# Taking the first 32 gathers of a two-layer graph network from the raw features instead of the normalised table

## The chip, the cores and the metric

The kernel runs on one core of one Trainium2 chip. The metric is the device time of one execution in microseconds; lower is better.

## The reference

The inputs are node features x (12500 nodes, 32 features, float32) and 200000 edges, each a source `src` and a destination `dst`, sorted by `dst`. Two residual layers follow each other. Cut to what matters:

```python
h = maximum(layernorm(x), 0)              # eps 1e-5, no gain
out_norm = rsqrt(maximum(count of src, 1))
in_norm  = rsqrt(maximum(count of dst, 1))
agg = segment_sum((h * out_norm[:, None])[src], dst)
x = x + agg * in_norm[:, None] @ W + b

h = maximum(layernorm(x), 0)
a = concat([h[dst], h[src] - h[dst]]) @ W1 + b1     # then relu,
m = relu(relu(relu(a) @ W2 + b2) @ W3 + b3) @ W4 + b4
x = x + segment_sum(m, dst) / maximum(count of dst, 1)
```

The edge attributes are not used.

## The kernel before

**Edges and chunks.** Edges lie in tiles of 128 (one per partition), and four tiles make a chunk of 512 edges (`TPC`, line 34); there are 391 chunks. `src_i` holds the source numbers, one column per tile (line 151), and `dst_i` the destinations. A row of a table is fetched for each edge of a tile by one indirect DMA on POOL, which takes one column of numbers (the helper `gather`, lines 247 to 250). POOL starts these in the order of the program, and does little else.

**Opening (lines 154 to 243).** x is loaded in four pieces of 32 nodes per partition on SP's queue, while ACT's queue loads `src_i`, `dst_i` and the small inputs. POOL makes constants. DVE normalises each piece (lines 228 to 242: sum, mean, difference, square, variance, with the root on ACT), and SP writes it to the table `tab_h` in DRAM, which has a 33rd column of ones. Its rows start at 48 (`OFF`), so that the numbers used for it are `src_j`, the sources plus 48.

**Degrees and early gathers (lines 279 to 361).** The out-degree of each node is counted on PE, in 196 batches of eight tiles, from one-hot matrices that DVE compares into being (lines 318 and 335). The table with the normalisation by out-degree, `tab_hn`, can only be written after that (lines 346 to 356). So that POOL is not idle meanwhile, the first 64 chunks (`EARLY`, line 57) are gathered from `tab_h`, without the out-degree: 256 gathers into `rows_early`, let go chunk by chunk as the batches go by (lines 324 to 330).

**First layer (lines 581 to 777).** Chunks 64 to 299 are gathered from `tab_hn` (944 gathers, tile `rows`, eight buffers of a chunk each) and summed by destination on PE with one-hot matrices (`sum_rows`). The last 91 chunks are not gathered: their edges are counted into matrices and multiplied with `tab_hn` held on the chip (`count_edges`, `multiply`). The 64 early chunks come in between: `scale_rows` (lines 631 to 667) is a generator that is advanced once per iteration of the loop over m (line 754), and a new one is begun every third iteration. Its stages are: load of a row of numbers; a one-hot on DVE; a matmul that looks up the factors 1/sqrt(degree) (line 643); four masked sums on DVE that pick the factor of each edge (line 650), the multiplication with `rows_early` (line 654) and the split into three bfloat16 terms; then the sum by destination. When a block of nodes has all its sums, `update_nodes` (lines 450 to 506) forms the new x and the second layer's tables `tab_i` and `tab_j`.

**Second layer (lines 782 to 926).** 1563 gathers from `tab_j` (tile `gj`) feed the four matmul layers on pairs of chunks. They can start when `tab_j` is complete.

**Order.** The engines' queues are filled in program order (the schedule is manual). Indirect DMAs take turns over eight completion semaphores, so that the ninth waits until the first has landed.

Of the kernel before, what the change touches and what calls it, by code (L numbers as in the profile page):

```python
# [8 lines left out]
F32 = mybir.dt.float32  # L9
# [3 lines left out]
AF = mybir.ActivationFunctionType  # L13
OP = mybir.AluOpType
AX = mybir.AxisListType

P = 128
N_NODES = 12500
N_EDGES = 200000
D = 32  # L20
HID = 64
EPS = 1e-5
# [3 lines left out]
OFF = 48  # L26
# [7 lines left out]
TPC = 4  # L34
CHUNK = TPC * P
NCH = -(-N_EDGES // CHUNK)
NTR = -(-N_EDGES // P)
NT = NCH * TPC
# [14 lines left out]
HG, HT = 2, 4  # L53
AHEAD_HG = 3


EARLY = 4 * GRP * J
LATER = 3
QE = EARLY // (GRP * J)

# [20 lines left out]
def gnn_kernel(  # L83
# [20 lines left out]
    nc = tc.nc  # L104
# [24 lines left out]
    def parts(rows):  # L129

        return rows.rearrange("(p j) c -> p j c", p=NPART)
# [6 lines left out]
    rows_early = early.tile([P, EARLY, TPC, D + 1], F32, name="rows_early")  # L138
# [12 lines left out]
    src_i = mp.tile([P, NT], I32, name="src_i")  # L151
# [4 lines left out]
    pieces = [slice(j, j + PC) for j in range(0, P, PC)]  # L156
    for at in pieces:
        nc.sync.dma_start(xp[:, at, :], parts(xa)[:, at, :])
    nc.scalar.dma_start(src_i, src_t)
    nc.scalar.dma_start(dst_i, dst_t)  # L160

    o = dst.offset + DIR * CHUNK
# [41 lines left out]
    nc.scalar.dma_start(w1s[D:, :HID], b1.rearrange("(o c) -> o c", o=1))  # L204
    nc.gpsimd.memset(w1s[D:, HID:], 0.0)

    fixed = ctx.enter_context(tc.tile_pool(name="fixed", bufs=1, space=bass.MemoryType.PSUM))
# [18 lines left out]
    for at in pieces:  # L228
        h, a = hx[:, at, :D], xp[:, at, :]
        m = fp.tile([NPART, PC], F32, name="la_m", bufs=2)  # L230
# [7 lines left out]
        sd = fp.tile([NPART, PC], F32, name="la_sd", bufs=2)  # L238
# [4 lines left out]
        nc.sync.dma_start(parts(tab_h[OFF:, :])[:, at, :], hx[:, at, :])  # L243
    first.close()
    src_j = stay.tile([P, NT], I32, name="src_j")

    def gather(tile_ap, table, col):
        nc.gpsimd.indirect_dma_start(  # L248
            out=tile_ap, out_offset=None, in_=table,
            in_offset=bass.IndirectOffsetOnAxis(ap=col, axis=0))  # L250

    def gather_chunk(rows, table, g):
        for t in range(min(TPC, NTR - g * TPC)):
            c = g * TPC + t
            gather(rows[:, t, :], table, src_j[:, c : c + 1])
# [23 lines left out]
    with tc.tile_pool(name="deg", bufs=3) as hp, tc.tile_pool(  # L279
        name="deg_ps", bufs=1, space=bass.MemoryType.PSUM  # L280
# [28 lines left out]
        nc.scalar.activation(turned_hi, hi_ps, AF.Copy)  # L309
        nc.sync.dma_start(hi_row.rearrange("(b t) e -> t b e", t=P), turned_hi.rearrange("t (b e) -> t b e", e=P))  # L310
        deg_ps = pp.tile([P, PART], F32, name="deg_ps")
        gathered, batches = 0, list(range(0, NTR, HG * HT))

        def one_hots(name, k, width, b):

            hot = hp.tile([P, HG, width, HT], BF16, name=name)
            n = min(HG, (NT - b) // HT)
            nc.vector.tensor_tensor(
                hot[:, :n], hl[:, k, b : b + n * HT].rearrange("p (g t) -> p g t", t=HT)[:, :, None, :].to_broadcast(
                    [P, n, width, HT]), lane_g[:, None, :width, :].to_broadcast([P, n, width, HT]), op=OP.is_equal)  # L320
            return hot

        for b in batches:
            to = min(EARLY, -(-EARLY * (b // (HG * HT) + AHEAD_HG) // len(batches)))
            if to > gathered:
                c = slice(gathered * TPC, to * TPC)
                nc.vector.tensor_scalar(src_j[:, c], src_i[:, c], OFF, None, op0=OP.add)
                for g in range(gathered, to):
                    gather_chunk(rows_early[:, g], tab_h[:, :], g)
                gathered = to  # L330
            hi = one_hots("hi", 0, PART, b)
            lo = one_hots("lo", 1, P, b)
            for t in range(b, min(NTR, b + HG * HT)):
                g, i = divmod(t - b, HT)
                nc.tensor.matmul(deg_ps, lo[:, g, :, i], hi[:, g, :, i], start=(t == 0), stop=(t == NTR - 1))
        nc.vector.tensor_scalar(src_j[:, EARLY * TPC :], src_i[:, EARLY * TPC :], OFF, None, op0=OP.add)
        deg = hp.tile([P, PART], F32, name="deg", bufs=1)
        nc.scalar.activation(deg, deg_ps, AF.Copy)
        turned = pp.tile([PART, P], F32, name="turned")
# [2 lines left out]
        sd = hp.tile([PART, P], F32, name="sd", bufs=1)  # L342
# [3 lines left out]
        for at in pieces:  # L346
            h = hx[:PART, at, :D]
# [77 lines left out]
    with tc.tile_pool(name="flag", bufs=1) as fp, tc.tile_pool(  # L425
        name="flag_ps", bufs=1, space=bass.MemoryType.PSUM
# [154 lines left out]
    with tc.tile_pool(name="e0", bufs=8) as sp, tc.tile_pool(name="nu", bufs=1) as np_, tc.tile_pool(  # L581
        name="direct", bufs=1) as dp, tc.tile_pool(name="e0_ps", bufs=1, space=bass.MemoryType.PSUM) as pp, tc.tile_pool(
        name="nu_ps", bufs=1, space=bass.MemoryType.PSUM) as np_ps:


        sums = Sums(np_, D3, "acc", (QE, QD, NQ - 1), (QE, QD), lambda q: ("_e", 2) if q < QE else ("_t", 3) if q < QD else ("_d", 3))
        hots, rows_of, group_ps, running, updates = {}, {}, {}, [], []
# [23 lines left out]
        def hot_ahead(g, name="hot", bufs=AHEAD + 4):  # L611
            hots[g] = one_hots(sp, rel_h[:, g * TPC : (g + 1) * TPC], W, name, bufs)

        def sum_rows(g):
            k, i = divmod(g, GRP)
            if i == 0:
                group_ps[k] = pp.tile([D3, SPAN], F32, name="ps_late" if g >= EARLY else "ps_early")
            ps, rows, hot = group_ps[k], rows_of.pop(g), hots.pop(g)
            for t in range(TPC):
                nc.tensor.matmul(  # L620
                    ps[:, STEP * i : STEP * i + W], rows[:, t, :], hot[:, t // 2, :, t % 2], start=(i == 0 and t == 0),
                    stop=(i == GRP - 1 and t == TPC - 1), skip_group_check=True)

        def add_rows(g):

            k, i = divmod(g, GRP)
            if i == GRP - 1:
                sums.add(slice(0, D3), P * k, group_ps.pop(k))
                added(range(k * GRP, (k + 1) * GRP))

        def scale_rows(g):

            row = sp.tile([PART, CHUNK], F16, name="srow", bufs=2)
            nc.sync.dma_start(row, bass.AP(
                tensor=hi_row.tensor, offset=hi_row.offset + g * CHUNK, ap=[[0, PART], [1, CHUNK]]))
            yield
            turned = sp.tile([PART, CHUNK], BF16, name="sturned", bufs=2)
            nc.vector.tensor_scalar(turned, row, part_s[:PART], None, op0=OP.is_equal)
            yield
            ps = pp.tile([P, TPC, P], F32, name="look")  # L640
            for t in range(TPC):
                for k in range(3):
                    nc.tensor.matmul(
                        ps[:, t, :], turned[:, t * P : (t + 1) * P], rn3[:, k], start=(k == 0), stop=(k == 2))
            yield
            w = factors[g % 2]
            for t in range(TPC):
                c = g * TPC + t
                mask = sp.tile([P, P], F32, name="mask", bufs=2)
                nc.vector.scalar_tensor_tensor(  # L650
                    mask, lanes_s, lo_early[:, c : c + 1], ps[:, t, :], op0=OP.is_equal, op1=OP.mult,
                    accum_out=w[:, t : t + 1])
            scaled = ps[:, 0, :].rearrange("p (t c) -> p t c", t=TPC)
            nc.vector.tensor_tensor(
                scaled, rows_early[:, g, :, :D], w[:, :, None].to_broadcast([P, TPC, D]), op=OP.mult)
            rows = rows_of[g] = sp.tile([P, TPC, D3], BF16, name="rows_scaled", bufs=2)
            nc.scalar.activation(rows[:, :, 3 * D :], rows_early[:, g, :, D:], AF.Copy)
            for k in range(3):
                part = rows[:, :, k * D : (k + 1) * D]
                nc.scalar.activation(part, scaled, AF.Copy)  # L660
                if k < 2:
                    nc.vector.tensor_sub(scaled, scaled, part)
            hot_ahead(g, "hot_e", 2)
            yield
            sum_rows(g)
            yield
            add_rows(g)


        table = dp.tile([P, PART, P], BF16, name="table")  # L670
# [111 lines left out]
    with tc.manual_schedule(), tc.tile_pool(name="prep", bufs=3) as prep, tc.tile_pool(name="e1", bufs=3) as ep, tc.tile_pool(name="fn", bufs=2) as fp, tc.tile_pool(  # L782
        name="p1_ps", bufs=2, space=bass.MemoryType.PSUM
# [146 lines left out]
    with tc.If(bad > 0):  # L930
        sums0 = dram.tile([NROW, D + 1], F32, name="sums0")
        sums1 = dram.tile([NROW, D], F32, name="sums1")
        with tc.tile_pool(name="gp", bufs=1) as gp, tc.tile_pool(name="ge", bufs=1) as ge, tc.tile_pool(
            name="ge_ps", bufs=1, space=bass.MemoryType.PSUM
# [108 lines left out]
            c = gp.tile([P, NBLK], F32, name="g_c")  # L1043
# [39 lines left out]
```

## Time and profile before

| What | Value |
|---|---|
| Median of 3 runs | 4330.28 us (4326.65 to 4355.74) |
| The profiled execution | 3552.55 us |
| Its span, first to last instruction | 3550.7 us |
| POOL busy | 2616.8 us (74%) |
| PE busy | 2630.5 us (74%) |
| DVE busy | 1669.8 us (47%) |
| ACT busy | 1103.2 us (31%) |
| Mean granted TensorE clock | 0.812 |
| First gather of `tab_h` starts | 48.56 us |
| First gather of `tab_hn` starts | 375.85 us |
| First gather of `tab_j` starts | 1572.77 us |
| Last gather starts | 3517.76 us |

The profile shows one execution, which was shorter than the timed runs. In it a line such as "L248 POOL DMA_INDIRECT" stands for the line of the kernel, the engine and the operation; then follow the tile that is written and what it is made from, the count, the busy time, the mean duration, and the idle time of the engine before it with what ended it. The line of all gathers is that of the helper, so they are told apart by their tiles.

### The profile page before, as it was taken

Reading aid. Unit: us, or ns where it says so; the run is one execution under the profiler, and the core shown is the slowest. Engines: PE = TensorE matmul, PEld = TensorE weight load, DVE = VectorE, ACT = ScalarE, POOL = GpSimd, SP = SyncE. Lnnn points to the kernel's source line nnn. Section 1 sums busy time; section 2 is a strip of 40 time slices with the busy share of each in tenths; the row PEclk is TensorE's granted clock in tenths of the full one; section 3 lists DMA queues with packets and bytes.
Section 4 is the critical chain, followed back from the end, with each engine's and each line's share of the span. In section 5 each row is a group of like instructions: output and inputs, shape, how many; then the busy total and the mean of one; then the engine's idle time right before and its main releaser. Section 6 shows DMA issues by size and latency. Waiting matters only on the chain. (4 is left out here: it accounts for less than half of the span.)

```text
span 3550.7 us, 50481 instructions
## 1 busy us (share of the span) xinstructions
PE 2630.5 (74%) x18596; PEld 1780.9 (50%) x18596; DVE 1669.8 (47%) x4150; ACT 1103.2 (31%) x2552; POOL 2616.8 (74%) x2782
## 2 busy tenths in 40 slices
PE   3871567777777777637888788877788877887787
PEld 2650355555555555514555555544455545554455
DVE  8995456667666665313333333333333333333333
ACT  0002355656656655301212222222212222222212
POOL 3777777777777777767777777777777777777775
PEclk9999998888888888657767877778867788778878
DMA  4113111111211111212222222222222222222221
GB/s 88 15 15 76 24 28 31 32 35 33 38 30 34 33 34 27 45 34 59 61 61 62 61 61 61 61 59 60 61 61 62 61 61 61 61 58 61 61 61 32
DMA packets 238327, 173.61 MB, mean 49 GB/s; under 512 B 157666, under 2 KB 186562, under 8 KB 238074
## 3 DMA queue, kind: packets, MB, share of 16 engines
q0 software_dynamic: 88416, 79.16, 12.4%
q1 hardware_dynamic: 131306, 85.26, 8.8%
q10 hardware_dynamic: 18352, 5.89, 0.9%
q8 instruction: 150, 2.46, 0.3%
q14 instruction: 103, 0.84, 0.1%
HBM read 157.18 MB, written 12.92 MB: 48 GB/s over the span
## 5 line engine op out<-in xcount | busy, mean ns | idle before, releaser
L248 POOL DMA_INDIRECT gj<-tab_j,src_j x1563 | 1474.9, 944 | 493.8 <-issue 414.8
L248 POOL DMA_INDIRECT rows<-tab_hn,src_j x944 | 891.8, 945 | 287.7 <-issue 200.5
L742 ACT ACTIVATE count<-count_ps 128x429 bf16<-128x429 f32 x1089 | 545.0, 525 | 368.7 <-PE count_ps L741 347.1
L845 PE MATMUL p<-ident,gj 128*128 128x128 f32 x784 | 243.6, 351 | 400.6 <-DMA gj<-tab_j,src_j 398.8
L878 DVE TENSOR_TENSOR h<-p,b3n 128x512 f32<-128x512 f32 x196 | 135.3, 690 | 811.5 <-PE p L875 811.5
L875 PE MATMUL p<-w3s,h 128*128 128x64 f32 x3128 | 483.0, 319 | 0.0
L875 PEld LDWEIGHTS p<-w3s,h 128*128 128x128 f32 x3128 | 453.9, 231 | 50.2 <-issue 41.2
L866 ACT ACTIVATE h<-p,b2s 128x512 f32<-128x512 f32 x391 | 247.3, 683 | 739.5 <-PE p L863 739.5
L741 PE MATMUL count_ps<-oh,lo 128*128 128x429 bf16 x1089 | 433.1, 409 | 47.2 <-ACT count L742 33.1
L845 PEld LDWEIGHTS p<-ident,gj 128*128 128x128 f32 x784 | 118.0, 161 | 662.4 <-issue 641.4
L696 PEld LDWEIGHTS <-table 128*128 128x128 bf16 x4508 | 352.3, 109 | 132.2 <-issue 74.8
L696 PE MATMUL st<-count,table 128*128 128x104 bf16 (+1 forms) x4508 | 414.9, 233 | 0.1
L620 PE MATMUL ps_late<-hot,rows 128*97 128x128 bf16 x944 | 166.3, 255 | 306.7 <-DMA rows<-tab_hn,src_j 243.7
L893 PEld LDWEIGHTS ps<-hot,h 128*64 128x64 f32 x3126 | 277.5, 193 | 170.1 <-issue 157.0
L248 POOL DMA_INDIRECT rows_early<-tab_h,src_j x256 | 246.7, 964 | 124.4 <-issue 53.3
L853 ACT ACTIVATE h<-p 128x512 f32<-128x512 f32 x196 | 117.0, 597 | 689.4 <-PE p L849 689.4
L849 PE MATMUL p<-turned,ai 128*64 128x512 f32 x782 | 322.3, 915 | 0.0
L893 PE MATMUL ps<-hot,h 128*64 128x128 f32 x3126 | 306.4, 361 | 0.5 <-DVE h L878 0.5
L685 DVE TENSOR_TENSOR oh<-keys,kept 128x858 bf16<-128x858 f16 x546 | 291.7, 590 | 7.0 <-PE count_ps L741 6.9
L620 PEld LDWEIGHTS <-rows 128*97 128x97 bf16 x944 | 103.5, 138 | 361.5 <-DMA rows<-tab_hn,src_j 293.3
L863 PE MATMUL p<-h,w2s 64*128 64x512 f32 x782 | 263.9, 755 | 0.0
L829 DVE TENSOR_TENSOR turned<-row,kept 128x512 f32<-128x512 f16 x391 | 249.8, 680 | 25.1 <-PE p L849 20.3
(186 smaller groups left out, 2426.2 us busy)
## 6 DMA issues: line engine op xcount, KB each, us to landing
row<-rel_row SPq DMA_DIRECT2D x195, 256.0 KB
gj<-tab_j,src_j POOLq DMA_INDIRECT x1563
rows<-tab_hn,src_j POOLq DMA_INDIRECT x944
ai<-tab_i SPq DMA_DIRECT2D x195, 64.0 KB
srow<-hi_row SPq DMA_DIRECT2D x64, 98.0 KB
rows_early<-tab_h,src_j POOLq DMA_INDIRECT x256
tab_j<-nu_aij SPq DMA_DIRECT2D x24, 128.0 KB
tab_i<-nu_aij SPq DMA_DIRECT2D x24, 128.0 KB
```

The costliest lines, as they stand in the source:

```text
L248: nc.gpsimd.indirect_dma_start(out=tile_ap, out_offset=None, in_=table, in_offset=bass.IndirectOffsetOnAxis(ap=col, axis=0))
L620: nc.tensor.matmul(ps[:, STEP * i : STEP * i + W], rows[:, t, :], hot[:, t // 2, :, t % 2], start=(i == 0 and t == 0), stop=(i == GRP - 1 ...
L685: nc.vector.tensor_tensor(oh[:, k, :n], keys[:, k, None, i : i + 2].to_broadcast([P, n, 2]), count_h[:, :n], op=OP.is_equal)
L696: nc.tensor.matmul(ps[:, : tiles * WD], table[:, h, :], c[:, :tiles, h, :], start=(h == 0), stop=(h == PART - 1))
L741: nc.tensor.matmul(ps[:, :n], lo[:, i % TPC // 2, :, i % 2], oh[:, k, :n, i % 2], start=True, stop=True)
L742: nc.scalar.activation(counts[g][:, t, a:b, :], ps[:, :n].rearrange("p (h d) -> p h d", d=WD), AF.Copy)
L829: nc.vector.tensor_tensor(turned, v["row"][:, k], part_f.to_broadcast([P, CHUNK]), op=OP.is_equal)
L845: nc.tensor.matmul(p1[:, t, :], v["gj"][:, t].rearrange("p k c -> p (k c)"), ident, is_transpose=True, start=(t == 0), stop=False, skip_gr ...
L849: nc.tensor.matmul(p1[k * HID : (k + 1) * HID].rearrange("p t e -> p (t e)"), v["ai"][:, k], v["turned"][k], start=False, stop=True, skip_ ...
L863: nc.tensor.matmul(p2s[k], w2s[s, :], v["h1"][s, :], start=True, stop=True)
L875: nc.tensor.matmul(p3[:, k * TPC + t, :], v["h2"][k][:, t * P : (t + 1) * P], w3s, start=True, stop=True)
L893: nc.tensor.matmul(ps[k * HID : (k + 1) * HID, o : o + W], v["h3"][:, k * TPC + t, :], v["hot"][k][:, t, :], start=(i == 0 and t == 0), st ...
```

## The change

The first eight chunks (32 gathers) are taken from x itself, `xa`, as soon as the first 32 columns of `src_i` are there, which are loaded by a DMA of their own. These gathers are put on POOL's queue behind its constants, ahead of all others. The remaining 56 early chunks are gathered from `tab_h` as before. What the raw rows lack, layer normalisation, is done edge by edge in `scale_rows`: the mean is taken off and the square formed in the stage of the one-hot, the variance and the root come in the stage of the matmul, and the reciprocal of the root is multiplied into the factor of the edge. The maximum with 0 is put into the multiplication, for all 64 early chunks.

```diff
+RAW = 8
...
-    nc.scalar.dma_start(src_i, src_t)
+    for c in (slice(0, RAW * TPC), slice(RAW * TPC, NT)):
+        nc.scalar.dma_start(src_i[:, c], src_t[:, c])
     nc.scalar.dma_start(dst_i, dst_t)
...
+    nc.gpsimd.memset(rows_early[:, :RAW, :, D:], 1.0)
+    for c in range(RAW * TPC):
+        gather(rows_early[:, c // TPC, c % TPC, :D], xa, src_i[:, c : c + 1])
...
-        gathered, batches = 0, list(range(0, NTR, HG * HT))
+        gathered, batches = RAW, list(range(0, NTR, HG * HT))
...
-            to = min(EARLY, -(-EARLY * (b // (HG * HT) + AHEAD_HG) // len(batches)))
+            to = min(EARLY, RAW + -(-(EARLY - RAW) * (b // (HG * HT) + AHEAD_HG) // len(batches)))
...
-        nc.vector.tensor_scalar(src_j[:, EARLY * TPC :], src_i[:, EARLY * TPC :], OFF, None, op0=OP.add)
+        for c in (slice(0, RAW * TPC), slice(EARLY * TPC, NT)):
+            nc.vector.tensor_scalar(src_j[:, c], src_i[:, c], OFF, None, op0=OP.add)
...
             nc.vector.tensor_scalar(turned, row, part_s[:PART], None, op0=OP.is_equal)
+            h = rows_early[:, g, :, :D]
+            if g < RAW:
+                m = sp.tile([P, TPC], F32, name="raw_m", bufs=2)
+                nc.vector.tensor_reduce(m, h, AX.X, OP.add)
+                nc.vector.tensor_scalar(m, m, 1.0 / D, None, op0=OP.mult)
+                nc.vector.tensor_sub(h, h, m[:, :, None].to_broadcast([P, TPC, D]))
+                square = sp.tile([P, TPC, D], F32, name="raw_sq", bufs=2)
+                nc.scalar.activation(square, h, AF.Square)
             yield
+            if g < RAW:
+                nc.vector.tensor_reduce(m, square, AX.X, OP.add)
+                nc.vector.tensor_scalar(m, m, 1.0 / D, EPS, op0=OP.mult, op1=OP.add)
+                sd = sp.tile([P, TPC], F32, name="raw_sd", bufs=2)
+                nc.scalar.activation(sd, m, AF.Sqrt)
...
-            nc.vector.tensor_tensor(
-                scaled, rows_early[:, g, :, :D], w[:, :, None].to_broadcast([P, TPC, D]), op=OP.mult)
+            if g < RAW:
+                nc.vector.reciprocal(m, sd)
+                nc.vector.tensor_tensor(w, w, m, op=OP.mult)
+
+            nc.vector.scalar_tensor_tensor(
+                scaled, h, 0.0, w[:, :, None].to_broadcast([P, TPC, D]), op0=OP.max, op1=OP.mult)
```

The definition of `gather` moves up with its first use.

More of the change, by code (lines that the diff above doesn't have):

```diff
@@ L205, in gnn_kernel, with gather @@
     nc.gpsimd.memset(w1s[D:, HID:], 0.0)
+    def gather(tile_ap, table, col):
+        nc.gpsimd.indirect_dma_start(
+            out=tile_ap, out_offset=None, in_=table,
+            in_offset=bass.IndirectOffsetOnAxis(ap=col, axis=0))
+    nc.gpsimd.memset(rows_early[:, :RAW, :, D:], 1.0)
+    for c in range(RAW * TPC):
+        gather(rows_early[:, c // TPC, c % TPC, :D], xa, src_i[:, c : c + 1])
     fixed = ctx.enter_context(tc.tile_pool(name="fixed", bufs=1, space=bass.MemoryType.PSUM))
@@ L245, in gnn_kernel @@
     src_j = stay.tile([P, NT], I32, name="src_j")
[L247 to L250, printed above, removed]
     def gather_chunk(rows, table, g):
```

## The prediction

> **What bounds the kernel now.** I read the page first: busy times and costliest groups.
>
> ```profile
> PE 2630.5 (74%) x18596; PEld 1780.9 (50%) x18596; DVE 1669.8 (47%) x4150; ACT 1103.2 (31%) x2552; POOL 2616.8 (74%) x2782
> ...
> L248 POOL DMA_INDIRECT gj<-tab_j,src_j x1563 | 1474.9, 944 | 493.8 <-issue 414.8
> L248 POOL DMA_INDIRECT rows<-tab_hn,src_j x944 | 891.8, 945 | 287.7 <-issue 200.5
> ...
> L248 POOL DMA_INDIRECT rows_early<-tab_h,src_j x256 | 246.7, 964 | 124.4 <-issue 53.3
> ```
>
> There are 2763 gathers. Each keeps POOL 0.94 us, and most of the idle time ahead of them is issue. POOL's list of waits (engine and line, what it waited for: total us, times, longest) shows where it truly waited:
>
> ```profile
> POOL rows_early L248 <- DMA b3n<-in_b: 44.2, 1, 44.2
> POOL gj L248 <- DVE turned L829: 17.8, 1, 17.8
> ```
>
> So there are two real gaps: 44.2 us before the first gather, 17.8 us before the second layer. Everything else runs at one pace: the rows gathers start from 375.85 to 1554.05 us, 943 steps, 1.249 us each (0.94 plus 0.30 of issue). POOL's stream sets the end, and a gather that moves into the first gap takes 1.249 us off, if nobody else becomes late. Next, the timeline of the opening (start, duration, engine, line):
>
> ```profile
> 4.22 0.14 POOL L205 MEMSET w1s<- 1x64 f32 x1
> ...
> 48.56 1.10 POOL L248 DMA_INDIRECT rows_early<-tab_h,src_j  x1 [44.20 <-DMA b3n<-in_b]
> ...
> 61.23 0.94 POOL L248 DMA_INDIRECT rows_early<-tab_h,src_j  x1 [2.84 <-DVE hi L318]
> ```
>
> POOL is free from 4.36 us. The gather at 48.56 needs `tab_h` and `src_j`. The ninth, at 61.23, waits 2.84 us: the built program has it wait for the landing of the first, which is late behind the 1.6 MB load of x for the residual. The timeline where the normalised table is written shows what DVE does to POOL:
>
> ```profile
> 267.82 1.23 DVE L355 TENSOR_TENSOR hx<-hx,terms 98x1024 f32<-98x1024 f32 x1 [1.15 <-ACT terms L353]
> 267.90 1.97 POOL L248 DMA_INDIRECT rows_early<-tab_h,src_j  x1 [0.30 <-issue]
> ...
> 270.17 0.94 POOL L248 DMA_INDIRECT rows_early<-tab_h,src_j  x1 [0.30 <-issue]
> 270.19 1.23 DVE L355 TENSOR_TENSOR hx<-hx,terms 98x1024 f32<-98x1024 f32 x1 [1.15 <-ACT terms L353]
> ```
>
> A gather that starts just behind L355 takes 1.97 us; one that starts just ahead of it takes 0.94. The four writes of `tab_hn` (L356, SP) are issued between 272.57 and 290.52 us. Last, the timeline around the seam to the first layer:
>
> ```profile
> 375.85 0.94 POOL L248 DMA_INDIRECT rows<-tab_hn,src_j  x1 [0.30 <-issue]
> ...
> 378.25 0.16 PEld L620 LDWEIGHTS <-rows 128*97 128x97 bf16 x1 [36.89 <-DMA rows<-tab_hn,src_j]
> ```
>
> PE has been waiting since 341.36 for rows that POOL cannot fetch before its early gathers are through. That wait is the cover for the change.
>
> **What the Trainium skill says.** "SBUF — State Buffer", section Who interferes with whom: a DVE instruction with two SBUF inputs contends with a GpSimd instruction that reads SBUF, so do the two-port modes of copies and tensor_scalar, and the one issued first goes ahead. The trace agrees: L355 has two SBUF inputs and delayed four of eight gathers, by 0.93 us on average; the gathers at L336 (tensor_scalar) and L368 (cast) lost 0.72 and 0.65; L348, whose second input is in PSUM, delays none. "DMA: Bandwidth & Descriptors", section Anatomy of one DMA: a fixed cost of about 2 us, mostly the receipt of the write. The trace has 2.4 us from the gather at 375.85 to PE's use at 378.25.
>
> **The change part by part.**
>
> Start of the raw gathers: POOL's constants end at 4.36, and the new memset of 32 elements is about 0.2 by the 0.32 of the memset of 128 (L175). The numbers' DMA is issued by about 1.2 us. Its landing isn't shown; the load of all of `src_i` had landed by 8.16, when ACT's L187, which waits for it, went on. Bounds 4.6 and 8.2; I take 5.2, as 16 KB need little beyond the fixed cost.
>
> The 32 gathers: 32 x 1.249 = 40.0 us. In the way are DVE's twelve two-input operations of 1.23 us (L233, L234, L241 for each of four pieces, 8.34 to 42.74). At L355's average (half of them, 0.93) that is 12 x 0.46 = 5.6. Of the four integer operations of 0.97 us (L300 to L303, 44.0 to 48.0) three still find raw gathers, 3 x 0.7 = 2.1. End: 5.2 + 40.0 + 7.7 = 52.9. Bounds: walking the gathers through DVE's intervals, with one let in between two operations that follow each other, gives 50.4; with none let in, 58.1. DVE lost nothing to gathers at 270.19, so I leave its chain as it is; if each of its sixteen operations waited 0.94, that is 15 us, which cover as below.
>
> So the first gather of `tab_h` starts at 52.9 instead of 48.56, 4.3 us late (1.8 to 9.5), with 32 fewer to do. The 2.84 us stall stays, as eight gathers still fall into the load of x; without it the gain grows by 2.8. POOL's gain: 40.0 - 4.3 = 35.7 us (30.5 to 41.0).
>
> Passing it on: the first rows gather moves from 375.85 to 340.2. `tab_hn` is ready at about 292.5 (290.5 plus the fixed cost), a cover of 47.7 us that holds the 15 us, too. `src_j` comes at one chunk in 196/56 x 1.09 = 3.8 us against POOL's 5.0. PE is ready at 341.36, the rows land at 342.6. From there POOL's stream is the same, and the 17.8 us before the second layer stay.
>
> Added work, eight times, at the durations of the same operations in the node update (L481 to L490): DVE two sums of 0.286, two scalings 0.170, one difference 0.293, one reciprocal 0.171, one product about 0.17, 1.55 us, 12.4 in all; ACT a Square 0.309 and a root 0.205, 4.1 in all. No table load comes with them: the built program has one, as before. The new multiplication costs what the old did (0.292 at L491 against 0.297 at L654). This falls into the first 120 us of the stage:
>
> ```profile
> 378.00:800.00 422.00, 306.41 (x3015) 226.59 (x3016) 259.61 (x820) 245.19 (x626) 319.00 (x339) 0.88 0.17 31
> ```
>
> (columns: PE, PEld, DVE, ACT, POOL busy). DVE is busy 62%, ACT 58%, so 12.4 and 4.1 us fit; without that cover they would cost 12 us. No rows gather took over 1.06 us, so small differences such as L484's cost POOL 0.11 at most, 0.9 in all; I take 0.
>
> Other queues: ACT's has one DMA more, 0.4 us before its wait to 8.16, hidden there. SP's has none more. In the built program new waits on the raw gathers stand at DVE's L429, before the first `srow` load on SP and at PE's matmul of L437, since `src_i`'s memory is reused; they ask for the first 32 landings only, some 260 us past. Cost 0.
>
> Sum: 3550.7 - 35.7 = 3515.0 of span, 3516.9 of the execution's 3552.55. The median of the runs, 4330.28, is 1.219 times that execution, and the profile doesn't say where the 778 us are. If the opening keeps its pace, the gain stays about 36; if everything is stretched alike, it is 43.5. I take 36: **4294 us**.
>
> **Rivals.** (1) The gain is hidden anyway. In the timed runs PE may be slower: its clock was 1.00 up to 378 us, 0.77 in the second layer. In the degree loop PE needs 0.90 of each 1.09 us batch. If a batch takes over 1.33 us (47.7/196 more), rows wait for `tab_hn` instead of POOL; from 1.52 (83.3/196 more) nothing is left. Against it: the loop comes first, at full clock. Time 4330.
>
> (2) Everything is stretched: 4330.28 - 43.5 = 4287, or 4280 at the upper bound of the gain. For it: one factor explains the 778 us; against it: no view shows it.
>
> (3) Slower: the chain DVE, ACT, DVE, ACT, DVE in `scale_rows`. DVE is in order; if it waits for the Square or the root behind ACT's count copies, the one-hots behind it are late, then PE, then the row buffers. Spare are 8 buffers x 5.0 = 40 us and PE's own waits (243.7 less 36.1 of 1089 us, some 22 in 120 us). With x us lost per chunk, 8x must pass 62 to cost anything, 98 to eat the gain (x = 12), 141 for 1% (x = 18, 4373). Against it: the same pair in the node update costs DVE little:
>
> ```profile
> DVE nu_m L486 <- ACT nu_t L485: 22.7, 25, 4.3
> ```
>
> 0.9 us a time, and an iteration lies between the stages.
>
> (4) The raw gathers don't run ahead: numbers at 8.2 and DVE shutting POOL out, end near 62; gain 25 or less, 4305 to 4312.
>
> **How the numbers follow.** Main case 0.60 (4287 to 4300), hidden 0.19 (4310 to 4335), stretched 0.11 (4278 to 4287), slower 0.05, late start 0.05. The runs before spread over 29 us. Below 1% is about what a measurement of this kernel can tell from no change, and 1% is 43.3 us: faster takes the stretched case and a sixth of the main one, 0.21; slower 0.05; the rest, 0.74, is within 1%. The range 4272 to 4332 leaves out some 0.05 below and 0.14 above.
>
> **What would show it.** Raw gathers from about 5 us, some of 1.5 to 2 us; first gather of `tab_h` near 53; first rows gather near 340; PE's wait of 36.9 at L620 nearly gone; 17.8 kept. A rows gather later than 350, or PE waits that grow beside the raw chunks, would prove me wrong.

## The result and the profile after

The changed kernel takes 4297.46 us (median of 13 runs, 4289.65 to 4317.1), the kernel before 4329.29 us beside it (13 runs, 4315.13 to 4357.79). The ratio is 0.9929, 95% interval 0.9909 to 0.9948: some 32 us faster, where 36 were forecast.

One thing must be known to read what follows. The first profile of the kernel before took 3552.55 us, the timed runs 4330. In the experiments this gap went with the chip: on one chip all 35 runs of the kernel before, and the single one on another, took 3550 to 3558 us; on a third all 12 took 4347 to 4370, and the timed runs (4315 to 4358) are like these. The third chip was met for one pair of experiments only, so that it always has this pace isn't shown. I call them **the 3550 pace** and **the 4350 pace**. The profile that the prediction was worked from is at the first; the timed runs above, and the profile of the changed kernel that belongs to them, are at the second. That execution took 4293.07 us, its span is 4291.3 us, the mean granted clock 0.757. So what it shows against the first profile is the change and the pace together, and the experiments have to part them.

From its page, the busy times and the groups of the gathers (busy, mean ns of one | idle time before them and what ended most of it):

```profile
PE 2813.3 (66%) x18596; PEld 1846.0 (43%) x18596; DVE 1680.5 (39%) x4199; ACT 1108.3 (26%) x2568; POOL 2616.7 (61%) x2783
...
L211 POOL DMA_INDIRECT gj<-tab_j,src_j x1563 | 1474.5, 943 | 859.8 <-issue 443.6
L211 POOL DMA_INDIRECT rows<-tab_hn,src_j x944 | 890.7, 944 | 624.8 <-issue 234.2
...
L211 POOL DMA_INDIRECT rows_early<-tab_h,src_j x224 | 211.3, 943 | 151.6 <-DVE src_j L334 84.8
```

A gather still keeps POOL 0.94 us. But the idle time ahead of the rows gathers has gone from 287.7 to 624.8 us and that of the gj gathers from 493.8 to 859.8: at this pace POOL waits for others through both layers, and its share of the span is 61%, not 74%. The opening is as forecast. Its timeline on POOL (start, duration):

```profile
4.42 0.16 POOL L215 MEMSET rows_early<- 128x32 f32 x1
5.92 1.10 POOL L211 DMA_INDIRECT rows_early<-in_xa,src_i  x1 [1.33 <-DMA src_i<-in_src_t]
7.32 1.75 POOL L211 DMA_INDIRECT rows_early<-in_xa,src_i  x1 [0.30 <-issue]
...
51.00 0.94 POOL L211 DMA_INDIRECT rows_early<-in_xa,src_i  x1 [0.30 <-issue]
52.24 0.95 POOL L211 DMA_INDIRECT rows_early<-tab_h,src_j  x1 [0.30 <-DVE lo L325]
```

The gathers of x run from 5.92 us, some of them stretched to 1.6 to 1.9 us, and the first of `tab_h` starts at 52.24. POOL's list of waits (total us, times, longest) tells what happens at the seam to the first layer:

```profile
POOL rows_early L211 <- DVE src_j L334: 84.8, 17, 6.0
...
POOL rows L211 <- PE c_ps L451: 62.0, 1, 62.0
...
POOL gj L211 <- DMA row<-rel_row: 24.2, 1, 24.2
```

Two new things stand here. The early gathers of `tab_h` wait for their numbers, 84.8 us in all, so it is the degree loop that leads and not POOL; and the first gather of `tab_hn` waits 62.0 us after POOL is through with the early ones. The wait of 44.2 us in the opening is gone.

Names in the views of the 4350 pace need caution. A trace records the events of semaphores, the counters by which engines and DMAs tell each other that something is done, and from these events the views infer what ended a wait. The first profile holds 63128 such records, this one 20047; on the semaphores of the gathers they are 16.0 a gather there and 3.7 here. No instruction is missing at this pace (50481 in the first profile and in run 6 below, of the same kernel), but two thirds of the events are. So many waits at this pace are put down to "remote" (an event whose sender is not found) or "issue" (no event found), and a name alone proves little.

### The profile page after: what moved, and what is told of

Read it like the earlier page. It is cut to its first block, busy times and chain, and to the rows that moved or that the text cites. A ratio compares the mean times of both kernels' runs of the same rounds, so it can differ in the third digit from the quotient of the medians.

```text
span 4291.3 us, 50527 instructions
## 1 busy us (share of the span) xinstructions
PE 2813.3 (66%) x18596; PEld 1846.0 (43%) x18596; DVE 1680.5 (39%) x4199; ACT 1108.3 (26%) x2568; POOL 2616.7 (61%) x2783
## 4 chain that ended last, share of the span: by engine, by line
PE 31%; another core or an unknown queue 11%; issue 10%; POOL 6%; DVE 4%; ACT 1%; DMA 0%; ACTq 0%; DVEq 0%; POOLq 0%
PE p L900 8%; POOL gj L211 6%; PE p L888 6%; PE p L874 5%; PE ps L918 4%; PE p L870 3%; PE st L721 1%; PE count_ps L766 1%; DVE hot L575 1%; DVE h L903 1%; DVE turned L854 1%; ACT count L767 1%; PE kept L831 1%; PE ps_late L628 0%
## 5 line engine op out<-in xcount | busy, mean ns | idle before, releaser
L211 POOL DMA_INDIRECT gj<-tab_j,src_j x1563 | 1474.5, 943 | 859.8 <-issue 443.6
L211 POOL DMA_INDIRECT rows<-tab_hn,src_j x944 | 890.7, 944 | 624.8 <-issue 234.2
L766 PE MATMUL count_ps<-oh,lo 128*128 128x429 bf16 x1089 | 468.4, 442 | 384.4 <-issue 182.6
L721 PE MATMUL st<-count,table 128*128 128x104 bf16 (+1 forms) x4508 | 446.0, 243 | 9.0 <-issue 9.0
L888 PE MATMUL p<-h,w2s 64*128 64x512 f32 x782 | 388.2, 844 | 69.8 <-issue 68.5
L874 PE MATMUL p<-turned,ai 128*64 128x512 f32 x782 | 367.3, 842 | 52.4 <-issue 51.7
L918 PEld LDWEIGHTS ps<-hot,h 128*64 128x64 f32 x3126 | 240.1, 172 | 345.9 <-DVE h L903 219.5
L870 PE MATMUL p<-ident,gj 128*128 128x128 f32 x784 | 206.5, 362 | 168.1 <-issue 132.9
L342 PE MATMUL deg_ps<-hi,lo 128*128 128x98 bf16 x1563 | 175.6, 271 | 196.3 <-DVE lo L325 116.2
L211 POOL DMA_INDIRECT rows_early<-tab_h,src_j x224 | 211.3, 943 | 151.6 <-DVE src_j L334 84.8
L575 DVE TENSOR_TENSOR hot<-rel_h,kept 128x512 f32<-128x512 f16 x391 | 249.1, 678 | 0.0
L342 PEld LDWEIGHTS <-lo 128*128 128x128 bf16 x1563 | 131.0, 126 | 240.9 <-DVE lo L325 143.0
```

What stands on the lines that cost most here:

```text
L211: nc.gpsimd.indirect_dma_start(out=tile_ap, out_offset=None, in_=table, in_offset=bass.IndirectOffsetOnAxis(ap=col, axis=0))
L575: nc.vector.tensor_tensor(hot, rel_h[:, g * TPC : (g + 1) * TPC][:, :, None].to_broadcast([P, TPC, W]), lanes_f[:, None, :W].to_broadcast( ...
L721: nc.tensor.matmul(ps[:, : tiles * WD], table[:, h, :], c[:, :tiles, h, :], start=(h == 0), stop=(h == PART - 1))
L766: nc.tensor.matmul(ps[:, :n], lo[:, i % TPC // 2, :, i % 2], oh[:, k, :n, i % 2], start=True, stop=True)
L870: nc.tensor.matmul(p1[:, t, :], v["gj"][:, t].rearrange("p k c -> p (k c)"), ident, is_transpose=True, start=(t == 0), stop=False, skip_gr ...
L874: nc.tensor.matmul(p1[k * HID : (k + 1) * HID].rearrange("p t e -> p (t e)"), v["ai"][:, k], v["turned"][k], start=False, stop=True, skip_ ...
```

## The experiments

Two theories were set against each other at first. Theory 1 is the main case of the prediction: POOL's stream sets the end and the head start shortens it. Its rival, theory 2, is the first rival of the prediction: at the pace of the timed runs rows wait for something else than POOL, and the head start is worth nothing. Which pace a run would have could not be chosen.

**1. The kernel before, once more.** No edit; it asks for the pace of an ordinary run.

> The kernel before, unchanged, for a second profile of it, since the profile of the change (span 4291 us) has stalls on PE marked as issue that the first profile of before (3551 us) has not. Both theories expect a span near 4325 us if the first profile was the odd one, with a degree loop longer than 214 us, and the first gather of tab_hn well after 376 us, waiting for tab_hn. Theory 1 (the early place of the 32 gathers makes the gain, through POOL's stream) expects POOL to be still busy with early gathers when tab_hn is ready. Theory 2 (the gain is made elsewhere) expects POOL to wait for tab_hn already here.

Measured: 3550.7 us, span 3548.9; first gather of `tab_h` at 48.5, of `tab_hn` at 374.5, of `tab_j` at 1570.8; the degree loop from 49.3 to 262.8. It shows no wait of a gather for `tab_hn`. The first profile was therefore no odd execution; it is what this chip does each time.

**2. The gathers of x without the head start.** The 32 gathers are started where the first of `tab_h` starts in the kernel before; all added work stays.

```diff
-    for c in range(RAW * TPC):
-        gather(rows_early[:, c // TPC, c % TPC, :D], xa, src_i[:, c : c + 1])
...
+        raw_j = hp.tile([P, RAW * TPC], I32, name="raw_j", bufs=1)
+        nc.vector.tensor_scalar(raw_j, src_i[:, : RAW * TPC], 0, None, op0=OP.add)
+        for c in range(RAW * TPC):
+            gather(rows_early[:, c // TPC, c % TPC, :D], xa, raw_j[:, c : c + 1])
         for b in batches:
```

> The change with its 32 raw gathers made to wait for a copy of their numbers, which DVE writes where the first early gathers were let go before (about 48 us): all added work stays, the head start is gone. Theory 1 (the head start on POOL makes the gain): as before, 4329 us, ratio 1.000 to 1.004. Theory 2 (the gain comes from something else that the change brings, such as the degree loop or the stages after it): about 4297 us, ratio 0.993.

Measured, at the 3550 pace: 3554.77 us against 3553.15 before, ratio 1.0005 (0.9997 to 1.0014). The gathers of x run from 50.4 us, the first of `tab_hn` starts at 376.6. With the head start taken away nothing is left of the gain, and with all the added work in place nothing is lost: the work that normalises edge by edge costs at most 0.14%, the upper end of the interval, some 5 us.

**3. All gathers of `tab_h` let go at once.** Only the pacing of the early gathers by the degree loop is taken away.

```diff
-AHEAD_HG = 3
+AHEAD_HG = 200
```

> The change with all numbers of the 56 early chunks made at the start of the degree loop, so that POOL is never held back there (it waited 85 us for them in the profile of the change) and has its early gathers done near 340 us instead of 415. Theory 1: another gain of some tens of us (ratio 0.98 to 0.985) if POOL's stream sets the first layer's start. Theory 2: no further gain, ratio 0.993, since tab_hn is written only near 475 us and POOL then waits 135 us instead of 62.

Measured, at the 3550 pace: 3519.07 us, ratio 0.9904 (0.9889 to 0.9919). The first gather of `tab_hn` starts at 337.9. At this pace the pacing by the loop costs POOL next to nothing, as the prediction's 3.8 us a chunk against POOL's 5.0 has it. The expectation starts from the waits of 85 us at the other pace, and was not tried there.

**4. The head start without the added work.** The three blocks that normalise the raw chunks in `scale_rows` are left out, so this kernel leaves out the normalisation of the first eight chunks.

```diff
-            if g < RAW:
+            if False:
```

> The change without the edge-wise layer normalisation of the first eight chunks (it leaves that computation out): prices the work that the change adds on DVE and ACT. Both theories: within 0.1% of the change, ratio 0.992 to 0.993, since 12 us on DVE and 4 on ACT lie beside other work.

Measured, at the 3550 pace: 3521.38 us, ratio 0.9906 (0.9891 to 0.9921), no better than the kernels that do the work (runs 3 and 8). Its timeline at the seam, to be read against the one of before, where the gather started at 375.85 and PE had waited 36.89 us:

```profile
340.35 0.94 POOL L211 DMA_INDIRECT rows<-tab_hn,src_j  x1 [0.30 <-ACT count L767]
...
343.50 0.16 PEld L628 LDWEIGHTS <-rows 128*97 128x97 bf16 x1 [0.99 <-DMA rows<-tab_hn,src_j]
```

POOL goes from the early gathers to those of `tab_hn` without a pause (0.30 us, as between any two), at 340.35, and PE waits 0.99 us in place of 36.89. Against run 1 that is 34.1 us earlier, 32.6 at the first gather of `tab_j` (1538.2 against 1570.8), and 28.7 in the span of these two single executions; the medians differ by 31.8. At this pace the main case of the prediction holds.

**5 and 6. The changed kernel and the kernel before, unchanged.** This pair fell on a chip of the 4350 pace.

> The change, unchanged. The first batch ran on a chip where the kernel before takes 3553 us, and POOL was never held up there. If this run meets that pace: first gather of tab_h near 52, first gather of tab_hn near 340, span near 3516, ratio 0.990 to 0.991. If it meets the pace of the result (before 4329): ratio 0.993 again. Theory 1 (the head start on POOL makes the gain) and its rival differ in the next run and not here.

> The kernel before once more, for its profile at the pace of the timed result if this chip has it. Theory 1 then expects POOL in the kernel before to come to the first gather of tab_hn some 30 us later than in the change (about 507 against 476.9 us), though the change itself waited 62 us there; its rival (at that pace the gain is made after or beside the early gathers) expects about the same start, 470 to 485 us, with a shorter wait of POOL, and the 31 us to come later.

Measured: 4334.81 us (after) against 4360.13 (before), ratio 0.9942 (0.9923 to 0.9961); the profiled one of the kernel before took 4356.41. The milestones of five executions, from their traces (us):

| Kernel | Degree loop | First gather of `tab_hn` | First gather of `tab_j` | Span |
|---|---|---|---|---|
| before (run 1), 3550 pace | 49.3 to 262.8 | 374.5 | 1570.8 | 3548.9 |
| head start alone (run 4), 3550 pace | 50.5 to 263.6 | 340.4 | 1538.2 | 3520.2 |
| before (run 6), 4350 pace | 49.3 to 451.7 | 509.4 | 1999.5 | 4354.6 |
| after (run 5), 4350 pace | 50.4 to 429.5 | 487.5 | 1978.4 | 4340.5 |
| after (profile of the result), 4350 pace | 50.0 to 418.9 | 476.9 | 1954.6 | 4291.3 |

The loop is read from its matmuls (ns of one: lowest, median, highest; start of the first and of the last). Run 1, run 6 and run 5:

```profile
L335 PE MATMUL deg_ps<-hi,lo x1563: 267/271/277, 49.3 to 262.5; 128*128 128x98 bf16 x196
...
L335 PE MATMUL deg_ps<-hi,lo x1563: 267/271/278, 49.3 to 451.4; 128*128 128x98 bf16 x196
...
L342 PE MATMUL deg_ps<-hi,lo x1563: 267/271/278, 50.4 to 429.3; 128*128 128x98 bf16 x196
```

At the 4350 pace the degree loop takes 402.4 us in place of 213.5, with matmuls of the same length, and POOL's waits are those of the result in both kernels. The kernel before:

```profile
POOL rows_early L248 <- DVE src_j L327: 83.3, 19, 7.6
...
POOL rows L248 <- DMA srow<-hi_row: 61.9, 1, 61.9
```

and the changed one on the same chip:

```profile
POOL rows_early L211 <- DVE src_j L334: 91.7, 17, 6.1
...
POOL rows L211 <- PE c_ps L451: 65.9, 1, 65.9
```

So the early gathers are no longer what the rows wait for, before the change nor after it: theory 2's wait is there. Its price is not. The first gather of `tab_hn` starts 57.7 us after the loop's end before and 58.0 after, which is one and the same chain; and the loop itself is 23.3 us shorter (402.4 to 379.1), which comes back as 21.9 at the first gather of `tab_hn` and 21.1 at the first of `tab_j`. The median gains 25.3. The spans of these two executions differ by 14.1 only; single ones tell little here, since the two traces of the changed kernel at this pace lie 49.2 us apart (4340.5 and 4291.3). The start at 509.4 is where theory 1 had put it for the kernel before (about 507), but not for its reason: POOL is through with its early gathers at 447.5 before and 421.5 after, and then waits 61.9 and 65.9 us. So its stream is not what sets the start, and theory 1 fails at this pace, too.

The name of what released that gather needs care. For the kernel before the profile says `srow<-hi_row`, but that load was issued at 508.72 and the gather started at 509.43. In the built program the first rows gather waits for the four writes of `tab_hn`, for an early gather's landing, and, since the rows' buffers take over memory of the set-up, for the last matmul of the set-up, `c_ps` (L443 before, L451 after). The timeline of the changed kernel, in the profile of the result, points to the last:

```profile
475.75 0.40 PE L451 MATMUL c_ps<-w4s,b3w 64*128 64x32 f32 x1
...
476.89 0.94 POOL L211 DMA_INDIRECT rows<-tab_hn,src_j  x1 [62.01 <-PE c_ps L451]
```

The gather follows the end of that matmul by 0.74 us here; in runs 5 and 6 it comes 0.74 and 0.75 us after it. The records of the semaphores settle it: the last write of `tab_hn` had landed by 449.8 in the profile of the result, 460.4 in run 5 and 482.6 in run 6, and POOL's queue then waited on until the event of `c_ps` at 476.2, 486.7 and 508.7.

**Why is the loop shorter?** The groups of the one-hot `hi` in the loop (busy, mean ns | idle time before them and what ended it) hold the difference; "remote" and "issue" are waits that the trace can't name. The kernel before at the 4350 pace, from 52 to 452 us:

```profile
L318 DVE TENSOR_TENSOR hi<-hl,lane_g 128x784 bf16<-128x784 f16 x192 | 106.5, 555 | 182.9 <-remote 130.8 <-PE deg_ps L335 52.1
```

the changed one on the same chip, in the same window:

```profile
L325 DVE TENSOR_TENSOR hi<-hl,lane_g 128x784 bf16<-128x784 f16 (+1 forms) x193 | 107.1, 555 | 160.8 <-remote 85.5 <-PE deg_ps L342 62.6 <-issue 12.5
```

and the head start alone at the 3550 pace, from 60 to 452 us:

```profile
L325 DVE TENSOR_TENSOR hi<-hl,lane_g 128x784 bf16<-128x784 f16 x186 | 101.9, 548 | 0.0
```

The operation lasts the same, 0.55 us. At the 3550 pace DVE never waits ahead of it, at the 4350 pace 182.9 us with 256 gathers in the loop and 160.8 us with 224. That is 0.714 and 0.718 us for a gather, and the difference, 22.1 us, is nearly the loop's 23.3. Each kernel has one such trace on this chip, though, and the profile of the result has a loop 10.2 us shorter again (368.9) with the same 224 gathers. The timeline of the kernel before shows one such stall:

```profile
277.60 0.56 DVE L318 TENSOR_TENSOR hi<-hl,lane_g 128x784 bf16<-128x784 f16 x1 [2.29 <-PE deg_ps L335]
...
278.08 0.68 DVE L318 TENSOR_TENSOR lo<-hl,lane_g 128x1024 bf16<-128x1024 f16 x1
...
282.74 0.94 POOL L248 DMA_INDIRECT rows_early<-tab_h,src_j  x1 [0.30 <-issue]
284.66 0.56 DVE L318 TENSOR_TENSOR hi<-hl,lane_g 128x784 bf16<-128x784 f16 x1 [5.89 <-remote]
...
285.88 0.90 PE L335 MATMUL deg_ps<-hi,lo 128*128 128x98 bf16 x8 [6.16 <-DVE lo L318]
...
287.66 0.94 POOL L248 DMA_INDIRECT rows_early<-tab_h,src_j  x1 [3.97 <-DVE src_j L327]
```

DVE and PE both stand still for some 6 us while POOL runs its gathers to the last of a batch of twelve (282.74). One microsecond after that one ends, DVE goes on, and POOL then waits for the next numbers. This comes again every 18.7 us or so (the next such gather starts at 306), that is once in three chunks. From it I formed **theory G**: each gather that shares the degree loop stretches it, by about 0.7 us, and the change gains at this pace because it takes 32 of them out of the loop. Its rival, **theory L**, is that the loop is as long whatever POOL does.

**7. All gathers of `tab_h` behind the loop.**

```diff
         for b in batches:
-            to = min(EARLY, RAW + -(-(EARLY - RAW) * (b // (HG * HT) + AHEAD_HG) // len(batches)))
-            if to > gathered:
...
-        for c in (slice(0, RAW * TPC), slice(EARLY * TPC, NT)):
-            nc.vector.tensor_scalar(src_j[:, c], src_i[:, c], OFF, None, op0=OP.add)
+        nc.vector.tensor_scalar(src_j, src_i, OFF, None, op0=OP.add)
+        for g in range(RAW, EARLY):
+            gather_chunk(rows_early[:, g], tab_h[:, :], g)
```

> The changed kernel with all 224 gathers of tab_h behind the degree loop instead of between its batches (the computation is the reference's). Read from the span of the degree loop alone (first to last matmul into deg_ps). At the pace of the timed runs (before 4330 to 4360): theory G, each gather that shares the loop stretches it (402.4 us with 256 gathers, 369 to 379 with 224, so 0.7 to 1.0 us each): without any the loop takes 215 to 250. Theory L, the loop is as long whatever POOL does, and its 22 to 33 us came from elsewhere: 365 to 400. At the pace of the first profile of before (3553) both say 211 to 214. The whole time grows in every case, by some 100 us or more, as 224 gathers of 1.25 us come late.

Measured: 3724.24 us, again at the 3550 pace. The loop takes 208.9 us (50.4 to 259.3), the first gather of `tab_hn` starts at 543.2. G and L are not told apart. It does show what the stream of early gathers is worth when nothing covers it: 203 us later than in run 4, and 202 us of span longer (3722.5 against 3520.2).

**8. 64 gathers of x instead of 32.**

```diff
-RAW = 8
+RAW = 16
```

> RAW = 16: 64 gathers from x instead of 32, 192 of tab_h left. At the pace of the timed runs, theory G: another 22 to 33 us off the loop than the change took, so some 50 us in all, ratio 0.985 to 0.990. Theory L: no more than the change, 0.993 to 0.996. At the pace of the first profile, where POOL's stream sets the end and the first 44 us are filled already with 32 gathers: as with 32, 0.990 to 0.992, first gather of tab_hn near 340.

Measured, at the 3550 pace: 3516.91 us, ratio 0.9896 (0.9881 to 0.9912); first gather of `tab_hn` at 337.8. The interval overlaps those of runs 3 and 4: the idle opening holds no more than about 32 gathers, and more of them from x bring nothing that can be seen.

**9. One addition for all of `src_j`.** The edit puts the addition of run 7 ahead of the loop, and leaves the gathers in it.

```diff
+        nc.vector.tensor_scalar(src_j, src_i, OFF, None, op0=OP.add)
         for b in batches:
...
-                c = slice(gathered * TPC, to * TPC)
-                nc.vector.tensor_scalar(src_j[:, c], src_i[:, c], OFF, None, op0=OP.add)
...
-        for c in (slice(0, RAW * TPC), slice(EARLY * TPC, NT)):
-            nc.vector.tensor_scalar(src_j[:, c], src_i[:, c], OFF, None, op0=OP.add)
```

> The changed kernel with one DVE addition for all of src_j ahead of the degree loop instead of one for each chunk inside it; gathers stay where they are. Rival A, the additions on DVE (8 fewer in the loop after the change) made the loop shorter, 3 to 4 us each: without the other 56 the loop falls from 369-379 to below 230 at the pace of the timed runs. Theory G (the gathers do it): within 12 us of 369 to 379, or longer, as POOL is free to run its gathers ahead. At the pace of the first profile both say 205 to 214.

Measured: 3517.76 us, at the 3550 pace. The loop takes 208.9 us (51.3 to 260.2), exactly as long as in run 7, which has no gather in it. Here 166 gathers start within it; the others come after its end, as POOL needs until 338 us for all. At this pace, then, a gather costs the loop nothing, and the additions 4.2 us in all (213.1 in run 4). Whether the additions matter at the 4350 pace it doesn't say.

**10. The kernel of run 2 again.**

> The changed kernel whose 32 gathers of x start only at the degree loop, where the first gathers of tab_h start in the kernel before; once more, for a run at the pace of the timed runs. Theory G: all 256 gathers share the loop again, so the loop is as long as before (400 to 405 us) and the time within 0.3% of before. Theory L: the loop keeps the 369 to 379 of the change, ratio 0.993 to 0.996. At the pace of the first profile: 1.000 as in the first such run.

Measured: 3554.58 us, ratio 1.0004 (0.9996 to 1.0012), at the 3550 pace. It confirms run 2 and says nothing on G.

**11 and 12. The kernel of run 7 again, twice.**

> Once more the changed kernel with all 224 gathers of tab_h behind the degree loop, for a run at the pace of the timed runs (before 4330 to 4360); nothing new is expected at the other pace, where the loop took 209 us. Theory G, each gather that shares the loop stretches it by 0.7 to 1.0 us: the loop takes 215 to 250 us instead of 369 to 379. Theory L, the loop is as long whatever POOL does: 365 to 400.

> A third time the changed kernel with its 224 gathers of tab_h behind the degree loop, again for a run at the pace of the timed runs. The traces at that pace show stalls of DVE in the loop of 0.60 to 0.69 us for each gather that shares it (174 us with 256 gathers, 155 and 135 us with 224). Theory G, the gathers bring the stalls: stalls of over 1 us add up to less than 20 us and the loop takes 209 to 235 us. Theory L, they come on their own: 130 us or more of stalls, the loop 365 to 400. At the pace of the first profile: 209 us and no stalls, as in the two runs before, and the question stays open.

Measured: 3719.85 and 3726.86 us, both at the 3550 pace, the second on yet another chip; the loop takes 208.9 us in both. So theory G was never tried at the pace at which it would speak. That the loop's gain goes with the number of gathers rests on two numbers of gathers, 256 and 224, in three traces (the third is the profile of the result, with 149.5 us in the same window, 0.67 us a gather). It is argued, not shown; the reason why DVE and PE stall on that chip and not on the others stays open.

One rival to both theories was not tried: the recording of the trace. The stalls come where events are missing. In the degree loop run 6 has 1461 records of semaphore events and run 1 has 3384, for the same work; outside the stretched parts, in the opening, they have 536 and 547. A gather at the 3550 pace brings 16 events, more than any other instruction of the loop. So the 0.7 us for a gather could be a price of recording its events on that chip, and with it a part of the measured gain. Against it: in the opening of run 5 more than half of the events are missing, too (455, against 1024 in run 4), and its 32 gathers of x are not stretched by it (36.6 and 36.7 us of POOL). No run tells the two apart.

The plain changed kernel had no run at the 3550 pace; runs 3, 4, 8 and 9, which hold its head start, lie between 3516.91 and 3521.38 us (run 9 is a single execution; the intervals of the others overlap), so none of them is a better version that could be told from it.

## Why the prediction was right, and where it was not

**The time.** 4294 forecast, 4297.46 measured. The size is right, and the mechanism is the one that was forecast only at the 3550 pace. At the pace of the timed runs the same size comes by another way: on the chip where both kernels were profiled the trace has a loop shorter by 23.3 us, of 25.3 in the median, and why it is shorter was argued, not shown. The closeness of 36 and 32 is in part luck.

**POOL's stream.** Start of the raw gathers 5.2 forecast, 5.92 measured, inside the bounds. The load of their numbers, issued at 0.76, had landed only by 5.6: 4.9 us for 16 KB, more than the fixed cost of about 2 us, and little beyond it, that the prediction goes by. The section that the prediction names ("DMA: Bandwidth & Descriptors", Anatomy of one DMA, in the Trainium skill) gives that figure for DMAs issued by GpSimd; this load is one of ACT's. The 32 gathers keep POOL 36.6 us, 0.200 us more each than the 0.943 of the others, 6.4 us in all; 7.7 had been put in for DVE's operations with two SBUF inputs. The Trainium skill, "SBUF — State Buffer", Who interferes with whom, and the trace agree on that lock: the gather at 7.32, which takes 1.75 us, starts while DVE's L245, with two SBUF inputs, runs from 7.03 to 8.26. First gather of `tab_h`: 52.9 forecast, 52.24 measured. At the 3550 pace (run 4) the first gather of `tab_hn` moved by 34.1 us where 35.7 had been forecast (bounds 30.5 to 41.0), and to 340.4 where the forecast was 340.2. Runs 2 and 4 show that the head start alone makes this gain.

**The step that failed** is the cover: "`tab_hn` is ready at about 292.5 (290.5 plus the fixed cost), a cover of 47.7 us". I looked for new waits on the raw gathers in the built program, but took the first rows gather to wait for `tab_hn` alone. It waits for the set-up's last matmul as well, whose end lies at 321.7 us in run 4 (it starts at 321.08 and takes 0.63). With the 0.75 us that follow, the cover was 340.4 - 322.5 = 17.9 us, not 47.7. That was still enough at the 3550 pace, but the loop needs to be longer by only 17.9/196 = 0.09 us a batch, not 0.24, before the head start begins to be lost. At the 4350 pace a batch takes 2.05 us in place of 1.09, and the cover is gone.

**Rival 1** had the right wait, wrongly named: rows wait for the chain behind the loop. Its threshold, 1.52 us a batch, was passed, and by its price nothing should have been left. It left out that the early gathers and the loop might not be independent. The prediction took the loop's length as given in every case.

**Rival 2**, one factor for all, is out: the opening is not stretched. The first gather of `tab_h` starts at 48.5 us in run 1 and in run 6. The 800 us between the paces begin in the degree loop (189 us) and go on in both layers.

**Rival 3**, the chain in `scale_rows`: the added operations on DVE take 13.2 us in all (12.4 forecast) and on ACT 4.0 (4.1), and the cover was there. In the stage that the prediction took for its cover the engines are emptier at the 4350 pace, not fuller (PE, PEld, DVE, ACT, POOL busy, the windows of the changed kernel):

```profile
478.00:900.00 422.00, 251.09 (x2240) 183.66 (x2241) 216.36 (x677) 191.75 (x489) 261.91 (x278) 0.80 0.20 30
```

DVE is busy 51% of it and ACT 45%, against 62% and 58%. DVE's waits for the new chain:

```profile
DVE raw_m L657 <- ACT raw_sq L654: 6.3, 2, 3.3
...
DVE raw_m L657 <- issue: 0.9, 2, 0.6
```

7.2 us over eight chunks, 0.9 a chunk, where 18 would have made the kernel slower by 1%. **Rival 4** is out with the 52.24. The 17.8 us before the second layer were kept, 18.4 in run 4, and are 24.2 at the 4350 pace.

**The scale.** I knew that the profile and the timed runs differed by 778 us and that no view showed where. The first rival said in which part of the kernel this would matter, and the main case was nevertheless worked out at the pace of the profile alone.

## What to carry to other kernels

A gather moved into an idle opening is worth its full step only as long as the engine that gets it sets the end; ask for every wait of the first instruction behind the seam, those for reused memory too, and take the cover from the latest of them. Where the timed runs and the profile differ by a fifth, profile again until one execution has the pace of the timed runs, before a sum is trusted, and see whether that trace is whole before the name of a wait is.

## What the runs showed of the hardware

The same program takes 3550 to 3558 us on two chips and 4347 to 4370 on another. The granted clock is not enough to explain it: it was 1.00 in the degree loop in both cases, while the loop took 213.5 and 402.4 us. What differs are stalls of DVE and PE of 2 to 9 us between instructions whose own durations are unchanged (0.55 us for `hi`). They are absent in the opening and in the 28 us behind the loop in which `tab_hn` is made (PE is busy 1.1 us of it in run 6, and POOL not at all), and present in the degree loop, where PE and DVE work beside POOL's gathers; in the layers, too, much idle time of PE and POOL is put down to what the profile cannot name. In the same traces about two thirds of the semaphore events are missing (20054 records in run 6, 63159 in run 1); whether the recording makes the stalls or suffers with them is open. At the 3550 pace 166 gathers in the loop cost it nothing (208.9 us with and without).
